# One of four graph layers: the aggregation as single 64-row graphs instead of pairs of graphs

## The chip, the cores and the metric

The kernel runs on one core of a Trainium2 chip. The metric is the device time of one execution in microseconds (us), from 2361.05 to 2364.01 in three runs, median 2362.12. A second figure, the span, runs from the first to the last instruction in one profiled execution.

The engines are named as in the profile: PE is TensorE's matmul row and PEld its weight loads, DVE is VectorE, ACT is ScalarE, POOL is GpSimd, SP is the sync engine, which issues most DMAs.

## What is computed

128 graphs of 64 nodes with 256 features go through four layers. Each adds its result to its input and normalises every row. Layer 2, to which the change belongs, is this (shapes: 128 graphs, n = 64, d = 256):

```python
A_norm = A + jnp.eye(n, dtype=A.dtype)
deg = jnp.sum(A_norm, axis=0) + jnp.sum(A_norm, axis=1) - jnp.diagonal(A_norm)
dinv = jax.lax.rsqrt(deg)
A_hat = A_norm * dinv[:, None] * dinv[None, :]
agg = jnp.einsum('nm,bmd->bnd', A_hat, features)
x = agg.reshape(-1, d)
h = jax.nn.relu(_batchnorm(x @ W1.T + b1, g1, be1))
out = h @ W2.T + b2
out = _batchnorm(out, g2, be2)
```

The change concerns the einsum alone: all 128 graphs are multiplied by one and the same 64x64 matrix `A_hat`. Layer 0 is attention over the graph, layer 1 attention over 512 listed edges, layer 3 two graph convolutions and four small LSTMs. All are in fp32.

## The kernel before

**Tiling.** The 8192 rows (128 graphs x 64 nodes) are cut into `NQ = 16` blocks. A block is a tile `[128, 4, 256]`: four groups `c` of 128 rows, and each group holds two graphs, one in partitions 0 to 63 and one in 64 to 127. A 64x64 graph matrix is therefore stored twice, on the diagonal of a 128x128 tile with zeros elsewhere: `bd` for the adjacency, and `aht` (built at line 546) for the transpose of `A_hat`.

**Stages.** Layers 0 and 1 are pipelined over the blocks, together with the end of layer 1 and the aggregation of layer 2, from the start to about 640 us. In round `q` the loop at line 560 walks through eight graphs (`l1_graph`) and puts in between: layer 0 of block `q + 2` (`l0_a` to `l0_e`), the projections of layer 1 of block `q + 1` (`l1_t`, `l1_qv`), and for block `q - 3` the three steps `v_a`, `v_b`, `v_c`. After every second block `l1_softmax` runs. The last three blocks have their `v_a`, `v_b`, `v_c` between the first batches of layer 2's first matrix product (`up_block`, line 616). Then come layer 2's products and normalisations, to about 950 us, and layer 3.

**The three steps.** `v_a` applies the attention of layer 1; its matmuls (line 351) have 64 rows and 64 columns each, and so lie in one of four quadrants of TensorE's array. `v_b` projects (line 365), adds the input and normalises by VectorE and GpSimd (line 96) into `x2`. `v_c` is the aggregation of layer 2: for each half `k` of the features and each group `c`, a 128x128 piece of `x2` is the weight operand and `aht` is streamed past it (line 377). The result is feature-major: partitions are features, columns are rows of the block. Four matmuls fill one PSUM bank, and ScalarE copies it into `A[:, q, ..]` (line 378), from which line 616 later reads.

**Banks.** PSUM banks are handed out by `bank`. The name `m`, which `v_c` uses, has three banks, taken in turn by all steps above apart from those of `l1_graph`; so the first matmul into a bank waits until the copy of its former contents has been read out. Around `v_c` these readers are ScalarE's line 264 (`spad`, from the projection), line 265 (`v`) and line 220 (`eT`). After `v_c` the banks go to lines 252 and 255 (`l1_qv`).

**Order.** The program is written as above, but a scheduler in the framework orders each engine's instructions by its own model before they are emitted, so small groups can be interleaved or moved.

Of the kernel before, what the change touches and what calls it, by code (L numbers as in the profile page):

```python
# [11 lines left out]
AF = mybir.ActivationFunctionType  # L12
# [5 lines left out]
P = 128  # L18
NB = 128
N = 64  # L20
D = 256
KD = D // P
# [5 lines left out]
PQ = 4  # L28
QT = 512
# [11 lines left out]
def kernel(ctx: ExitStack, tc: tile.TileContext, i, out):  # L41
    nc = tc.nc
# [8 lines left out]
    A = main.tile([P, NQ, 2 * QT], F32, name="A")  # L51
# [61 lines left out]
    with ExitStack() as two:  # L113
# [8 lines left out]
        def bank(shape, name="m", bufs=3):  # L122
            return (psm if name == "m" else ps).tile([P] + shape, F32, name=name, bufs=bufs)
# [22 lines left out]
        aht = wa.tile([P, P], F32, name="aht")  # L146
# [224 lines left out]

        def v_c(q):
            x2 = L1.pop(q)["x2"]
            for k in range(KD):
                p_ = bank([PQ, P])
                for c in range(PQ):
                    nc.tensor.matmul(p_[:, c, :], x2[:, c, k * P:(k + 1) * P], aht, start=True, stop=True)  # L377
                nc.scalar.activation(A[:, q, k * QT:(k + 1) * QT], p_.rearrange("p c t -> p (c t)"), AF.Copy)

        class su:  # L380

# [45 lines left out]
        for h in range(HEADS):  # L427
            r, c0 = slice((h % 2) * 64, (h % 2 + 1) * 64), P - HEADS + h
# [44 lines left out]
        for r in range(EC):  # L473
            for c in range(EC):
                nc.tensor.matmul(pcol[:, r, :], perm[:, c, r * P:(r + 1) * P], col_f[:, c, :],
                                 start=c == 0, stop=c == EC - 1)
# [83 lines left out]
        for q in range(NQ):  # L560

            between = [
                [(l0_a, q + 2), (v_a, q - LAG)],
                [(l0_b, q + 2)],
                [(v_b, q - LAG), (l0_c, q + 2)],
                [(l1_t, q + 1)],
                [(l1_qv, q + 1, 0), (l0_d, q + 2)],
                [(v_c, q - LAG)],
                [(l1_qv, q + 1, 1)],
                [(l0_e, q + 2)],  # L570
            ]
            for b in range(GQ):
                some(l1_graph, q, b)
                for step, n, *more in between[b]:
                    some(step, n, *more)
            if q % BPS == BPS - 1:
                l1_softmax(q // BPS)
# [32 lines left out]
        def pbank():  # L610
            return pools[next(banks) % len(pools)].tile([P, QT], F32, name="pz")

        def up(q, m):
            p_ = pbank()
            for k in range(KD):
                nc.tensor.matmul(p_, w1[:, k, m * P:(m + 1) * P], A[:, q, k * QT:(k + 1) * QT],  # L616
                                 start=k == 0, stop=k == KD - 1)
            nc.vector.bn_stats(st1[:, m, q, :], p_)
            return p_
# [12 lines left out]
        q = 0  # L632
        for n in range(NQ - LAG, NQ):
            for step in (v_a, v_b, v_c):
                step(n)
                up_block(q)
                q += 1
# [30 lines left out]
        for q in ends:  # L668
            p_ = up(q, 3)
# [43 lines left out]
        for q in ends:  # L713
            p_ = pbank()
# [216 lines left out]
```

## Time and profile before

| | us |
|---|---|
| median of three runs | 2362.12 |
| the profiled execution's own time | 2363.15 |
| its span | 2361.3 |
| TensorE busy in it | 2239.4 |
| VectorE busy | 1019.8 |
| ScalarE busy | 910.8 |
| GpSimd busy | 408.1 |
| mean granted TensorE clock, as a share of full speed | 0.974 |

By stretches of the span, TensorE is busy 437 of 465 us between 180 and 645 us, 111 of 115 us between 645 and 760 us, and 1376 of 1411 us from 950 us to the end. Matmuls are pipelined: a record's duration is longer than its turn on the engine, so the pace of a group is better read from the distance between starts. An fp32 matmul leaves two records[...]. In the fences below, a timeline row gives start, length, engine, line, operation, output and inputs, rows*columns of the weights, the streamed operand and the number of records; a row of a line's own view gives minimum, median and maximum duration in ns, and first and last start; a row of waits gives the total, the number and the longest.

### The profile page before, as it was taken

To read this page: it belongs to the slowest core of one execution; us is meant where nothing else is said; L and a number is where in the kernel's file an instruction comes from. 1 tells how busy PE (TensorE), PEld (TensorE's weight loads), DVE (VectorE), ACT (ScalarE), POOL (GpSimd) and SP (SyncE) were. 2 spreads that over 40 slices of the span, in tenths; PEclk is the share of its full clock that TensorE was granted. 3 is DMA by queue.
4 is the path that set the end of the run, shared out by engine and by line. 5 is a ranking of instruction groups with operands and counts; after the bars stand their busy time and mean duration, and the time that the engine had idled before them with its cause. 6 is when DMAs were issued, how large, how long until landed. Compare 5 with 4: busy or idle time off the path is not lost.

```text
span 2361.3 us, 25955 instructions
## 1 busy us (share of the span) xinstructions
PE 2239.4 (95%) x9673; PEld 1541.9 (65%) x9673; DVE 1019.8 (43%) x2320; ACT 910.8 (39%) x1885; POOL 408.1 (17%) x531
## 2 busy tenths in 40 slices
PE   5999999999899996999999999999999999999996
PEld 3767787778654444568568568568568568568475
DVE  5676766776744434322422422422422422422322
ACT  2565665566433801333333333333333333323331
POOL 1013333223320001010210210210210210210101
PEclk8899999999999997999999999999999999999998
DMA  3020222122223003000100100100100100100100
GB/s 119 10 38 29 46 57 39 38 46 39 30 47 90 0 0 116 18 18 1 54 18 1 54 18 1 54 19 1 54 18 1 54 18 1 45 10 1 36 1 27
DMA packets 126797, 74.75 MB, mean 32 GB/s; under 512 B 81872, under 2 KB 117328, under 8 KB 126416
## 3 DMA queue, kind: packets, MB, share of 16 engines
q1 hardware_dynamic: 124032, 70.22, 12.1%
q10 hardware_dynamic: 1616, 1.84, 0.2%
q8 instruction: 76, 1.25, 0.2%
q0 software_dynamic: 1024, 1.05, 0.2%
q14 instruction: 49, 0.40, 0.1%
HBM read 44.51 MB, written 28.57 MB: 31 GB/s over the span
## 4 chain that ended last, share of the span: by engine, by line
PE 87%; DVE 6%; ACT 3%; DMA 2%; POOL 2%; issue 1%; SPq 0%; POOLq 0%; ACTq 0%; DVEq 0%
PE l L818 32%; PE l L824 18%; PE g L772 5%; PE pz L680 5%; PE pz L616 5%; PE e L277 3%; PE g L780 2%; PE m L252 2%; PE m L365 2%; PE m L187 2%; PE z L286 2%; PE m L255 2%; PE m L377 1%; PE m L166 1%; DVE lo L290 1%
## 5 line engine op out<-in xcount | busy, mean ns | idle before, releaser
L818 PE MATMUL l<-H,wih 128*128 128x256 f32 (+2 forms) x2496 | 801.1, 472 | 0.3 <-DVE H L789 0.2
L818 PEld LDWEIGHTS l<-H,wih 128*128 128x128 f32 x2496 | 467.3, 191 | 246.2 <-issue 158.8
L824 PE MATMUL l<-hid,whh 128*128 128x256 f32 (+2 forms) x1536 | 435.9, 437 | 0.0
L824 PEld LDWEIGHTS l<-hid,whh 128*128 128x128 f32 x1536 | 291.8, 190 | 128.4 <-issue 61.2
L830 ACT ACTIVATE gate_i<-l,bias 128x256 f32<-128x256 f32 (+2 forms) x176 | 100.3, 570 | 646.2 <-PE l L824 514.9
L833 DVE TENSOR_TENSOR gate_i<-gate_i,gate_g 128x256 f32<-128x256 f32 (+2 forms) x96 | 47.8, 498 | 571.1 <-ACT gate_g L830 571.1
L834 POOL TENSOR_TENSOR cell<-gate_f,cell 128x256 f32<-128x256 f32 (+2 forms) x96 | 83.7, 872 | 1018.2 <-ACT gate_f L830 1018.2
L290 DVE SCALAR_TENSOR_TENSOR lo<-z,hi 128x512 fp32r<-128x512 f32 x256 | 167.4, 679 | 63.2 <-ACT hi L289 62.2
L289 ACT ACTIVATE hi<-z 128x512 fp32r<-128x512 f32 x256 | 143.7, 598 | 102.6 <-PE z L286 98.6
L82 POOL TENSOR_TENSOR ln_rs<-ln_rs,mhalf 128x2 f32<-128x2 f32 (+1 forms) x96 | 86.8, 904 | 520.3 <-DVE ln_ng L94 520.2
L830 ACT ACTIVATE gate_g<-l,bias 128x256 f32<-128x256 f32 (+2 forms) x176 | 100.2, 570 | 108.1 <-PE l L818 59.0
L830 ACT ACTIVATE gate_o<-l,bias 128x256 f32<-128x256 f32 (+2 forms) x176 | 99.5, 565 | 71.4 <-PE l L824 54.0
L277 PE MATMUL e<-lo,apad 128*128 128x512 f32 x256 | 110.7, 432 | 14.0 <-DVE lo L290 14.0
L772 PE MATMUL g<-wg,hT 128*128 128x256 f32 x512 | 122.6, 384 | 0.0
L286 PE MATMUL z<-gath_r,qs 128*128 128x512 f32 x256 | 109.9, 481 | 8.1 <-DVE lo L290 8.0
L837 DVE TENSOR_TENSOR cell<-gate_i,gate_g 128x512 f32<-128x512 f32 (+2 forms) x80 | 48.4, 604 | 154.6 <-ACT gate_g L830 154.5
L772 PEld LDWEIGHTS g<-wg,hT 128*128 128x128 f32 x512 | 98.3, 194 | 23.7 <-issue 10.5
L616 PE MATMUL pz<-A,w 128*128 128x512 f32 x256 | 112.7, 596 | 0.0
L277 PE MATMUL e<-hi,apad 128*128 128x512 f32 x256 | 108.3, 423 | 2.4 <-ACT hi L289 2.3
L838 ACT ACTIVATE gate_g<-cell 128x256 f32<-128x256 f32 (+2 forms) x176 | 89.9, 511 | 51.3 <-DVE cell L837 36.8
L843 DVE TENSOR_TENSOR H<-gate_o,gate_g 128x512 f32<-128x512 f32 (+2 forms) x80 | 47.6, 595 | 106.1 <-PE l L818 90.1
L616 PEld LDWEIGHTS pz<-A,w 128*128 128x128 f32 x256 | 48.2, 191 | 56.2 <-issue 55.0
(197 smaller groups left out, 2798.5 us busy)
## 6 DMA issues: line engine op xcount, KB each, us to landing
xin<-in_x SPq DMA_DIRECT2D x16, 512.0 KB
ld<-table SPq DMA_DIRECT2D x16, 512.0 KB
x_dram<-x SPq DMA_DIRECT2D x16, 512.0 KB
x2r<-x_dram SPq DMA_DIRECT2D x32, 256.0 KB
x_dram<-A SPq DMA_DIRECT2D x64, 128.0 KB
x3r<-x_dram SPq DMA_DIRECT2D x64, 128.0 KB
out<-st SPq DMA_DIRECT2D x64, 128.0 KB
wih<-in_WihT SPq DMA_DIRECT2D x3, 1024.0 KB
```

The costliest lines, as they stand in the source:

```text
L82: nc.gpsimd.tensor_tensor(dst, dst, mhalf[:, :n], OP.pow)
L277: nc.tensor.matmul(pes[S], apad[:, k, P - HEADS - r0:2 * P - HEADS - r0], t, start=first and n == 0, stop=False)
L286: nc.tensor.matmul(z, L1[q]["qs"][c][:, s, k * P:(k + 1) * P], gath_r, start=True, stop=True)
L289: nc.scalar.activation(hi, z, AF.Relu)
L290: nc.vector.scalar_tensor_tensor(lo, z, 0.0, hi.bitcast(F32), op0=OP.max, op1=OP.subtract)
L616: nc.tensor.matmul(p_, w1[:, k, m * P:(m + 1) * P], A[:, q, k * QT:(k + 1) * QT], start=k == 0, stop=k == KD - 1)
L680: nc.tensor.matmul(p_, w2[:, k, m * P:(m + 1) * P], hidden(q, k), start=k == 0, stop=k == M1 - 1)
L772: nc.tensor.matmul(p_[:, c, :], hT[:, k, c * P:(c + 1) * P], wg[n][:, k, :], start=k == 0, stop=k == KD - 1)
L818: nc.tensor.matmul(gates[n], wih[p][:, k, mw * P:(mw + 1) * P], Hw[:, k, :, s, :], start=k == 0, stop=not s and k == KD - 1)
L824: nc.tensor.matmul(gates[n], whh[p][:, k, m * P:(m + 1) * P], hid[:, k], start=False, stop=k == KD - 1)
L830: nc.scalar.activation(act[n], gates[n], AF.Tanh if n == "g" else AF.Sigmoid, bias=bias[:, p - 1, m:m + 1])
L838: nc.scalar.activation(act["g"], cell[:, j], AF.Tanh)
```

## The change

In `v_c` each matmul over 128 rows (two graphs) becomes two over 64 rows (one graph each, `s = 0` in partitions 0 to 63, `s = 1` in 64 to 127), with the matching 64x64 block of `aht`. Weights are then 64 rows by 128 columns, and 64 columns are streamed. The results of the two halves go to two different banks: a bank now belongs to a graph half `s` and holds both feature halves, instead of belonging to a feature half `k`. Both banks are taken at the start. ScalarE copies each bank once, into runs of 64 elements of `A`, so that `A` has the same contents as before.

```diff
         def v_c(q):
             x2 = L1.pop(q)["x2"]
+
+            p_ = [bank([KD, PQ, N]) for _ in range(2)]
             for k in range(KD):
-                p_ = bank([PQ, P])
                 for c in range(PQ):
-                    nc.tensor.matmul(p_[:, c, :], x2[:, c, k * P:(k + 1) * P], aht, start=True, stop=True)
-                nc.scalar.activation(A[:, q, k * QT:(k + 1) * QT], p_.rearrange("p c t -> p (c t)"), AF.Copy)
+                    for s in range(2):
+                        r = slice(s * N, (s + 1) * N)
+                        nc.tensor.matmul(p_[s][:, k, c, :], x2[r, c, k * P:(k + 1) * P], aht[r, r],
+                                         start=True, stop=True)
+            dst = A[:, q, :].rearrange("p (k c s t) -> p s k c t", k=KD, c=PQ, s=2)
+            for s in range(2):
+                nc.scalar.activation(dst[:, s], p_[s], AF.Copy)
```

## The prediction

> **What bounds the kernel now.** I read the page first (busy shares, then the chain), then the waits of TensorE, then the changed line, then the timeline around single blocks.
>
> ```profile
> PE 2239.4 (95%) x9673; PEld 1541.9 (65%) x9673; DVE 1019.8 (43%) x2320; ACT 910.8 (39%) x1885; POOL 408.1 (17%) x531
> PE 87%; DVE 6%; ACT 3%; DMA 2%; POOL 2%; issue 1%; SPq 0%; POOLq 0%; ACTq 0%; DVEq 0%
> ```
>
> TensorE is the path: 87% of the chain, against 6% for VectorE. The change sits in the stage from 180 to 760 us; there the waits of TensorE, asked for that stretch, are these at the top:
>
> ```profile
> PE e L277 <- DVE lo L290: 12.0, 6, 2.0
> PE z L286 <- DVE lo L290: 6.6, 8, 1.0
> PE m L377 <- POOL x L96: 2.9, 3, 1.9
> ```
>
> Some 20 us of waits for VectorE in 580 us, in a few clumps of one or two microseconds after a softmax: everywhere else TensorE has work queued. So a microsecond of TensorE more or less in the changed block is nearly a microsecond of the kernel. The changed line itself:
>
> ```profile
> L377 PEld LDWEIGHTS m<-aht,x x256: 186/192/333, 199.8 to 731.1; 128*128 128x128 f32 x128
> L377 PE MATMUL m<-aht,x x256: 270/275/580, 199.8 to 731.2; 128*128 128x128 f32 x128
> ```
>
> 16 blocks of 8 fp32 matmuls; each matmul leaves two records (two passes), so 16 a block. The durations are latencies and overlap; the pace has to be read from the timeline. Three stretches of it:
>
> ```profile
> 59.16 3.54 PEld L475 LDWEIGHTS m<-A 128*128 128x128 f32 x31 [0.24 <-issue]
> 199.81 1.86 PEld L377 LDWEIGHTS m<-aht,x 128*128 128x128 f32 x16 [0.69 <-issue]
> ...
> 700.68 1.88 PE L616 MATMUL pz<-A,w 128*128 128x512 f32 x4
> 702.40 1.95 PE L377 MATMUL m<-aht,x 128*128 128x128 f32 x16
> 704.18 1.88 PE L616 MATMUL pz<-A,w 128*128 128x512 f32 x4
> ```
>
> Line 377's loads start every (1.86 - 0.19) / 15 = 0.111 us. Line 475 loads weights of the same shape and streams only two columns past them, and its loads start every (3.54 - 0.19) / 30 = 0.112 us. So 0.11 us is what loading 128 columns of fp32 weights costs; that streaming 128 columns costs about as much is hidden under it. A block holds TensorE for 704.18 - 702.40 = 1.78 us, 28.5 us in all.
>
> [...] there is one load of 64 rows by 128 columns, at line 526, mean 310 ns, beside 200 ns for 64 by 64 at line 522, both while the granted clock was low. [...] Line 351 of this kernel already uses four 64x64 quadrants[...]:
>
> ```profile
> 659.06 1.15 PE L351 MATMUL m<-am,v 64*64 64x64 f32 x32
> 660.14 1.13 PE L616 MATMUL pz<-A,w 128*128 128x512 f32 x2
> ...
> 684.78 1.88 PE L616 MATMUL pz<-A,w 128*128 128x512 f32 x4
> 686.59 1.16 PE L351 MATMUL m<-am,v 64*64 64x64 f32 x64
> 687.68 1.98 PE L616 MATMUL pz<-A,w 128*128 128x512 f32 x4
> ```
>
> At 659 us only the upper row half works: 32 records hold TensorE for 1.08 us. At 686 us both halves alternate: 64 records in 1.09 us. The second half runs for nothing, loads included. And the switch costs: four records of line 616 last 4 x 0.43 = 1.72 us, so line 351 could have begun at 686.50 and began at 686.59 (0.09); its 16 steps at half of 0.11 us are about 0.9 of the 1.09 us (0.2 over, at the first step and at the end); the group behind it takes 1.98 instead of 1.88 us (0.10), since no weights were loaded ahead. I take 0.35 us for a switch in and out: 0.1 in (nothing where the block waits anyway), 0.05 at the first step, 0.2 out.
>
> **The change part by part.**
>
> Removed and added on TensorE: per block 8 matmuls (128 rows, 128 weight columns, 128 streamed) become 16 (64 rows, 128 weight columns, 64 streamed). Streaming halves, but the load of 128 columns stays at 0.11 us a pass, and there are twice as many. With both row halves at work, 16 / 2 matmuls x 2 passes x 0.112 = 1.79 us: the same as the 1.78 now. The arithmetic saved was never what set the pace. Added for certain is the switch, 0.35 us a block.
>
> Moved: the banks. Before, the first bank is filled (0.9 us) and then the second; now the lower half needs the second bank at once. Program order on TensorE outside the block is unchanged, but inside it the scheduler of the new program places the matmuls thus: in the five blocks n = 1, 3, .. 9 three upper ones, then three lower ones that wait for ScalarE, then alternating; in n = 2, 4, .. 10 two and two; in n = 0 four and four; in n = 11 seven and seven; in 12 to 15 alternating throughout. [...] the lower half's eight matmuls (8 x 0.224 = 1.79 us, alone enough to fill the block) start only when the second bank is free and the upper ones ahead are issued. Everything behind in TensorE's queue (lines 252 or 286) waits with them. What frees the bank stands in ScalarE's rows:
>
> ```profile
> 244.43 2.02 PE L377 MATMUL m<-aht,x 128*128 128x128 f32 x16 [0.17 <-ACT v L265]
> ...
> 275.76 1.99 PE L377 MATMUL m<-aht,x 128*128 128x128 f32 x16
> 276.38 0.17 ACT L264 ACTIVATE spad<-m 64x4 f32<-64x4 f32 x1
> ```
>
> Times from each block's present start, and the delay of what follows:
> - n = 2, 4, .. 10: the bank is freed by line 264, at 276.55 - 275.76 = 0.79 us. Lower half from about 0.88, to 2.67, switch out 2.85; now 1.75. Delay 1.1 us, five times: 5.5.
> - n = 1, 3, .. 9: the bank is freed by line 220 at 0.34 us, but the third upper matmul is issued at about 0.46. 0.46 + 1.79 + 0.2 = 2.45; now 1.86 (244.43 to 246.29). Delay 0.6, five times: 3.0.
> - n = 0: fourth upper matmul at 0.74: 2.73 against 1.78. Delay 0.95. The bank (line 264, 0.54) is no limit.
> - n = 11: line 265 frees the bank at 1.34: 1.44 + 1.79 + 0.2 = 3.43 against 2.31. Delay 1.1.
> - n = 12: it waits for GpSimd's x2 rows anyway (2.9 us above), and the last row leaves five pairs as it now leaves five matmuls. 0.3 for the switch.
> - n = 13 to 15: both banks free, 0.35 each: 1.05.
>
> Sum 5.5 + 3.0 + 0.95 + 1.1 + 0.3 + 1.05 = 11.9 us.
>
> ScalarE: two copies out as before, now into 64-element runs. Line 355 has that very pattern and takes 597 ns, line 378 599 ns: nothing. They start when the whole block is done, so the first copy comes about 0.9 us later within the block; its bank is next wanted by line 255, 0.9 us behind the block in the odd blocks and more in the even ones, and it is free about then. I book nothing, with 0.2 us a block (3 us) as the upper bound. VectorE's, GpSimd's and SP's queues keep their order. A itself holds the same values in the same places.
>
> Back the other way: VectorE, the one behind which TensorE waits after each softmax, gains room while TensorE is late. Of 20 us of such waits a tenth may vanish; but what VectorE works on there comes from TensorE after the block, so it shifts along. I take 1 us off: +11 us. The profiled execution had a span of 2361.3 and a time of 2363.15, 1.0 above the median 2362.12; the delay is added to the median: 2373.
>
> **The rivals.**
> - *Loads of the two halves don't run together with 128 columns each.* Then a block is 32 x 0.112 = 3.6 us, plus the switch: 1.8 + 0.35 = 2.15 more, some 16 x 2.15 = 34 us: 2396. For it: line 351 loads only 64 columns a quadrant. Against it: there two quadrants per row half load side by side, so both halves already load all 128 columns at once.
> - *The pace is the streaming, not the load, with 64 rows* (0.056 us a pass): the lower half takes 0.9 instead of 1.79 us. Blocks 2, 4, .. 10 are then 0.2 later, 1, 3, .. 9 and 0 about 0.3 earlier, 11 0.2 later, 13 to 15 0.5 earlier, 12 even: 1.0 - 1.8 + 0.2 - 1.5 = -2 us, 2360: no change that can be told. For it: half the rows. Against: line 475 and the 310 ns of line 526.
> - *Faster.* On that pace, and with the second bank free before the block begins (the delay of TensorE lets ScalarE get its rows 220 and 264 done first, so the waits disappear), each block saves 1.78 - 0.93 - 0.35 = 0.5 us: -8 us, 2354. It decides from a load under about 0.08 us a pass; line 475 says 0.112.
> - *Nothing changes*: the delays of the first twelve blocks vanish in the waits behind VectorE, only the switches of the last four are left, +2 us. Against: those waits sit right behind the softmax, 10 us and more after the block, on work that TensorE feeds.
>
> **How the numbers follow.** My case 0.73, 2373, with its own range 2367 to 2381: the switch 0.2 to 0.5 us a block, the copies up to 3 us, a third of the delay absorbed, and where the low-clock windows fall (from 364 to 377 us the mean granted clock is 0.87, which costs 13 x 0.13 = 1.7 us; one more or less is as much). Serial loads 0.08, 2396. Streaming pace 0.09, 2360. Faster 0.03, 2354. Absorbed 0.07, 2364. For eight in ten I reach from 2364, which takes in the absorbed case, to 2388, part of the way to the serial one; the streaming and the faster case and most of the serial one, 0.19, are left out. What can be told from no change is 0.2%, 4.7 us: slower 0.81 (my case and the serial one), same 0.16 (streaming and absorbed), faster 0.03.
>
> **What would show it.** Right: records of the new matmul line 32 a block, 64*128, starting in pairs every 0.11 us; a block of 2.2 to 2.9 us; a gap in front of the first lower matmul in n = 2, 4, .. 10; mean load still about 190 ns; line 384's copies near 599 ns. Wrong: pairs every 0.06 us or single records every 0.11 us, or TensorE's waits behind lines 290 shrinking by as much as the blocks grow.

## The result and the profile after

The changed kernel takes 2378.5 us (median of 4 runs, 2377.72 to 2379.75) against 2361.97 us before (4 runs): 16.5 us more, a ratio of 1.0069 with a 95% interval from 1.0052 to 1.0087. The forecast was 2373, the range 2364 to 2388. The profiled execution has a span of 2377.9 us, 16.6 more than before.

First the page after the change, with the busy times and the chain that ended last:

```profile
PE 2253.8 (95%) x9929; PEld 1552.5 (65%) x9929; DVE 1019.5 (43%) x2320; ACT 912.8 (38%) x1885; POOL 407.9 (17%) x531
PE 87%; DVE 6%; ACT 3%; POOL 2%; DMA 2%; issue 1%; SPq 0%; POOLq 0%; ACTq 0%; DVEq 0%
```

TensorE is busy 14.4 us longer and still carries 87% of the chain; the other engines have the same busy time within 2 us. So the loss shows on TensorE itself. Its changed line (durations in ns: minimum, median, maximum):

```profile
L380 PEld LDWEIGHTS m<-aht,x x512: 182/188/330, 199.1 to 746.7; 64*128 64x128 f32 x171
L380 PE MATMUL m<-aht,x x512: 272/272/472, 199.1 to 746.7; 64*128 64x64 f32 x171
```

Twice the records (32 a block), each as long as before: a load with half the rows takes 188 ns, where a full one took 192. A block between two rounds' work and one among line 622's matmuls (the former line 616), from the timeline of the changed kernel (start, length, and so on as explained above; other rows left out):

```profile
277.55 0.40 PE L277 MATMUL e<-lo,apad 128*128 128x512 f32 x1
...
277.88 0.52 PEld L380 LDWEIGHTS m<-aht,x 64*128 64x128 f32 x4 [0.36 <-issue]
277.88 2.72 PE L380 MATMUL m<-aht,x 64*128 64x64 f32 x32
...
278.39 0.17 ACT L264 ACTIVATE spad<-m 64x4 f32<-64x4 f32 x1
...
278.61 1.86 PEld L380 LDWEIGHTS m<-aht,x 64*128 64x128 f32 x28 [0.21 <-ACT spad L264]
...
280.53 0.50 PE L286 MATMUL z<-gath_r,qs 128*128 128x512 f32 x1
...
690.06 1.86 PEld L380 LDWEIGHTS m<-aht,x 64*128 64x128 f32 x32 [0.76 <-POOL x L96]
690.06 2.00 PE L380 MATMUL m<-aht,x 64*128 64x64 f32 x32
...
691.99 0.30 PEld L622 LDWEIGHTS pz<-A,w 128*128 128x128 f32 x2
```

In the one at 690 us both halves run side by side: 32 loads in the same 1.86 us in which line 377 did 16, a load every (1.86 - 0.19) / 31 = 0.054 us, so one every 0.108 us in each half. In the one at 277 us, two upper matmuls (4 records) are issued, then TensorE stands until ScalarE's line 264 has emptied the second bank at 278.56. The six upper matmuls still to come, whose bank is free, don't pass the waiting one: no load of the block starts between the fourth record and 278.61. The lower half starts at 278.61 with all its 16 passes still to do, and sets the end.

The waits of TensorE in the stretch from 180 to 775 us (total, number, longest):

```profile
PE e L277 <- DVE lo L290: 12.0, 6, 2.0
PE z L286 <- DVE lo L290: 7.7, 8, 1.3
PE m L380 <- POOL x L96: 2.9, 3, 2.0
```

The second was 6.6 us before, in a stretch of nearly the same length: it grew by 1.1, where I had taken 1 off. Last, the granted clock right behind softmaxes, by windows of 8 us (columns: window, length, busy time and records of PE, PEld, DVE, ACT and POOL, then PEclk, DMA share, GB/s). Three of the kernel before, then the corresponding three of the changed one:

```profile
292.00:300.00 8.00, 7.00 (x21) 5.18 (x22) 7.82 (x12) 3.04 (x6) 3.22 (x5) 0.57 0.22 66
370.00:378.00 8.00, 7.76 (x35) 5.56 (x35) 7.91 (x11) 4.49 (x8) 1.80 (x3) 0.79 0.20 68
...
520.00:528.00 8.00, 6.56 (x18) 4.85 (x19) 7.82 (x11) 2.80 (x5) 3.65 (x5) 0.57 0.22 66
```

```profile
294.00:302.00 8.00, 6.00 (x19) 4.19 (x18) 7.82 (x11) 2.96 (x6) 4.49 (x5) 0.57 0.23 64
372.00:380.00 8.00, 6.00 (x18) 4.12 (x16) 7.82 (x11) 2.96 (x6) 4.54 (x5) 0.57 0.24 65
...
529.00:537.00 8.00, 6.22 (x17) 4.54 (x18) 7.82 (x12) 2.80 (x5) 3.99 (x5) 0.57 0.27 66
```

The clock's records in these two traces hold only the shares 1 and 0.5, so a PEclk of 0.79 is a half-speed stretch of 3.4 us in the window ((1 - 0.79) x 2 x 8), and 0.57 one of 6.9 us. Behind the six softmaxes between 200 and 640 us the kernel before has two long ones and four short ones, the changed kernel five long ones and one short one.

### The profile page after: what moved, and what is told of

The parts are those of the page before. It is cut to its first block, busy times and chain, and to the rows that moved or that the text cites. A ratio compares the mean times of both kernels' runs of the same rounds, so it can differ in the third digit from the quotient of the medians.

```text
span 2377.9 us, 26465 instructions
## 1 busy us (share of the span) xinstructions
PE 2253.8 (95%) x9929; PEld 1552.5 (65%) x9929; DVE 1019.5 (43%) x2320; ACT 912.8 (38%) x1885; POOL 407.9 (17%) x531
## 4 chain that ended last, share of the span: by engine, by line
PE 87%; DVE 6%; ACT 3%; POOL 2%; DMA 2%; issue 1%; SPq 0%; POOLq 0%; ACTq 0%; DVEq 0%
PE l L824 32%; PE l L830 18%; PE pz L622 5%; PE g L778 5%; PE pz L686 5%; PE e L277 4%; PE g L786 2%; PE m L252 2%; PE m L365 2%; PE m L187 2%; PE z L286 2%; PE m L255 2%; PE m L380 2%; PE m L228 1%; PE m L166 1%
```

## The experiments

The theory: the load of 128 weight columns sets the pace, so halving rows and streamed columns saves nothing; the loss is the switch of tiling (0.35 us a block) plus the delay of the lower half by the order and by the second bank's wait. The rivals: streaming sets the pace; the halves don't overlap; the loss is the clock's.

**1. What TensorE time in the block is worth (`dose3`).** The kernel before, with the block's first matmul issued three more times.

```diff
-                    nc.tensor.matmul(p_[:, c, :], x2[:, c, k * P:(k + 1) * P], aht, start=True, stop=True)
+                    for _ in range(4) if c == 0 and k == 0 else range(1):
+                        nc.tensor.matmul(p_[:, c, :], x2[:, c, k * P:(k + 1) * P], aht, start=True, stop=True)
```

> The kernel before, with three full-size matmuls of the aggregation repeated in each of the 16 blocks (same bank, same result; no row tiling, same bank order). TensorE gets 16 x 3 x 0.224 = 10.7 us of work, about what the change added to its blocks (10 us). Theory A, that a lengthened round also lengthens the windows of low granted clock behind the softmax: more than the dose, 2374 to 2381 us, and the low-clock time between 140 and 760 us rises from 34 us towards the 51 us of the changed kernel. Theory B, that the excess belongs to the row tiling itself: the dose alone, 2372 to 2373 us, low-clock time about 34 us.

Measured: 2372.12 us against 2362.73, ratio 1.0039 [1.0024, 1.0053]. 3 matmuls x 2 passes x 0.111 x 16 blocks are 10.7 us; 9.4 arrived. So a microsecond in the block is nearly one of the kernel, and this longer round brought no further loss: between 140 and 770 us the clock was low for 31 us (34 in the kernel before, 51 in the changed one).

**2. The switch alone (`switch1`).** The kernel before with one extra matmul of 64 rows ahead of each block, whose result is overwritten.

```diff
+                if k == 0:
+                    nc.tensor.matmul(p_[:, 0, :N], x2[:N, 0, :P], aht[:N, :N], start=True, stop=True)
```

> The kernel before, with one extra 64-row matmul (64 rows, 128 weight columns, 64 streamed) ahead of each block's first matmul, whose result the block then overwrites. If a switch of the tiling mode in and out costs about 0.35 us: 16 x (0.22 + 0.35) = 9 us more, about 2371 us or somewhat above. If the switch costs nothing and the matmul its two passes alone: 16 x 0.22 = 3.6 us more, about 2365.5 us.

Measured: 2370.5 us, 7.8 more than before (1.0032 [1.002, 1.0045]). Its timeline around one block:

```profile
276.70 0.40 PE L277 MATMUL e<-lo,apad 128*128 128x512 f32 x1
277.02 0.43 PE L377 MATMUL m<-aht,x 64*128 64x64 f32 x2
277.39 2.05 PE L379 MATMUL m<-aht,x 128*128 128x128 f32 x16
```

The block begins 0.32 us after the last matmul ahead of it (0.23 to 0.24 where no switch lies between, as in experiment 5), and the full-row matmuls start 0.37 later: 0.22 for the extra matmul's two passes and 0.15 for the way in and out. The whole 7.8 us are 0.49 a block: 0.22 for the two passes and 0.27 for the switch. The switch is real; its size here is a little below the 0.35.

**3. Quadrants (`quad`).** The changed kernel with each matmul cut again, into two of 64 weight columns, in the same banks and the same place.

```diff
-                    for s in range(2):
-                        r = slice(s * N, (s + 1) * N)
-                        nc.tensor.matmul(p_[s][:, k, c, :], x2[r, c, k * P:(k + 1) * P], aht[r, r],
-                                         start=True, stop=True)
+                    for j in range(2):
+                        for s in range(2):
+                            r = slice(s * N, (s + 1) * N)
+                            f0 = k * P + j * N
+                            nc.tensor.matmul(p_[s][j * N:(j + 1) * N, k, c, :], x2[r, c, f0:f0 + N], aht[r, r],
+                                             start=True, stop=True)
```

> The changed kernel with each 64-row matmul cut once more, into two of 64 weight columns, in the four quadrants of the array; banks and waits as in the changed kernel. If the load of 128 columns sets the changed kernel's pace, a pass now takes 0.056 us in each quadrant: the last three blocks fall from 2.1 to about 1.3 us, the blocks that wait for their second bank by 0.9 us, in all 16 x 0.85 = 13 us less than the changed kernel or a little more with the clock windows, 2360 to 2365 us. If a matmul has a fixed cost of about 0.11 us a pass whatever its columns, no gain: 2378 us.

Measured: 2365.42 us, ratio to before 1.0013 [1.0004, 1.0022]; 13 us less than the changed kernel. The same arithmetic, the same streams of 64 columns, twice the instructions; only each load is of 64 columns instead of 128 (median 135 ns, 188 in the changed kernel). Its timeline shows the same wait for line 264, and the rest in 1.15 us instead of 1.9:

```profile
276.06 0.44 PE L382 MATMUL m<-aht,x 64*64 64x64 f32 x6
276.79 1.15 PE L382 MATMUL m<-aht,x 64*64 64x64 f32 x58 [0.29 <-ACT spad L264]
277.87 0.73 PE L286 MATMUL z<-gath_r,qs 128*128 128x512 f32 x2
```

The pace was the load of 128 columns. "Streaming sets the pace" falls.

**4. One half after the other (`apart`).** The changed kernel with all eight upper matmuls ahead of the eight lower ones (the loop over `s` outermost).

> The changed kernel with the order turned: all eight matmuls of the upper half, then all eight of the lower half, so that the halves never work side by side. If the halves overlap in the changed kernel and the load sets the pace: a block takes 16 x 0.224 + 0.35 = 3.9 us, 34 us above the kernel before, 2396 us, or up to 2402 with longer low-clock windows. If they hardly overlap in the changed kernel: about the changed kernel's 2378 us.

Measured: 2402.61 us (2398.38 to 2414.27), 1.0184 [1.0158, 1.0209]. Serial halves cost 24 us more than alternating ones (2378.5), so in the changed kernel they do overlap. (The clock is low for 58 us here against 51 there, which at half speed explains 3.4 of the 24 us at most.) Not foreseen was where the clock gave way: see experiment 7.

**5. Another place (`late_before`, `late_after`, `late_quad`).** In each round `v_c` is called two slots later, where its banks have long been free; the same edit to the kernel before, to the changed one, and to the one with quadrants.

```diff
-                [(v_c, q - LAG)],
+                [],
                 [(l1_qv, q + 1, 1)],
-                [(l0_e, q + 2)],
+                [(v_c, q - LAG), (l0_e, q + 2)],
```

> The kernel before, with its step v_c called two slots later in each round (directly ahead of l0_e instead of after the second graph batch): same matmuls, other place. It is the yardstick for the next two. If the place costs nothing by itself, 2362 (2359 to 2365). If the rows that v_c follows there keep TensorE waiting, or if what came after v_c lacks its cover, up to 2370.

> The changed kernel with v_c at that later place, where both banks are free long before the block. Theory 'the second bank's wait makes two thirds of the loss, the tiling switch one third': the upper half no longer runs alone, each block costs only a switch more, 16 x 0.35 = 5.6 us above late_before, that is about 2368 and 8 to 11 us below the changed kernel. Rival 'the loss is the halves themselves (loads of 128 columns by one half don't keep the pace of 0.111 us, or the clock gives way after blocks of half rows)': the place doesn't matter, 14 to 17 us above late_before, about 2378.

> As late_after, but each matmul cut again into two of 64 weight columns, so that four quadrants of TensorE work. Load time a block 32 x 2 passes / 4 quadrants x 0.056 = 0.9 us instead of 1.79 plus the switch of 0.35: 0.5 us less a block than late_before, 8 us in sum: 2354 if late_before is at 2362, faster than both kernels. Rival 'the quadrants' gain is taken back at the next wait for VectorE': 2360 to 2362.

Measured against 2361.55 before: `late_before` 2356.82 (0.998 [0.9971, 0.9988]), `late_after` 2363.88 (1.001 [1.0002, 1.0018]), `late_quad` 2355.99 (0.9975 [0.9965, 0.9985]).

The place alone gains 4.7 us, which I had not expected of the control. The waits of `late_before` in the same stretch say where from:

```profile
PE e L277 <- DVE lo L290: 12.0, 6, 2.0
PE z L286 <- DVE lo L290: 3.6, 9, 0.5
PE m L377 <- POOL x L96: 2.9, 3, 1.9
```

Line 286's wait for VectorE falls from 6.6 to 3.6 us, and line 377's wait for ScalarE's `v` (1.5 us before) is gone: 4.5 us in sum. The tally isn't exact: line 187 now waits 1.2 us for VectorE, line 351's waits fall by 0.8, and the clock is low for 3.4 us less.

At this place the change costs 7.1 us (5.6 were expected) instead of 16.5, 0.44 a block. The timelines of `late_before` and of `late_after` around the same block:

```profile
322.50 0.39 PE L277 MATMUL e<-lo,apad 128*128 128x512 f32 x1
322.73 1.95 PE L377 MATMUL m<-aht,x 128*128 128x128 f32 x16
324.51 0.81 PE L228 MATMUL m<-wh,eT 128*128 128x256 f32 x3
```

```profile
323.57 0.40 PE L277 MATMUL e<-lo,apad 128*128 128x512 f32 x1
323.90 2.00 PE L380 MATMUL m<-aht,x 64*128 64x64 f32 x32
325.83 1.99 PE L228 MATMUL m<-wh,eT 128*128 128x256 f32 x8
```

From the last matmul ahead to the first behind it is 2.01 us and 2.26 us: 0.25 more, and the switch is all of it. No matmul waits for a bank. So 9.4 of the 16.5 us belong to the old place: to the order inside the block, the second bank's wait, and what hangs on them. About 6 of them are in the blocks themselves (without block 12, the change adds 9.8 us to them at the old place and 3.7 here); most of the rest is the clock's, as experiment 7 shows. No run tells the order and the wait apart. "The place doesn't matter" (2378) falls.

With quadrants the same stretch takes 1.62 us:

```profile
323.41 0.40 PE L277 MATMUL e<-lo,apad 128*128 128x512 f32 x1
323.73 1.16 PE L382 MATMUL m<-aht,x 64*64 64x64 f32 x64
325.03 1.99 PE L228 MATMUL m<-wh,eT 128*128 128x256 f32 x8
```

That is 0.39 less than `late_before`, 6.2 us over 16 blocks, and yet the two kernels can't be told apart: this expectation missed. In the two profiles, line 286's waits for VectorE are 1.0 us longer (4.6), line 351's for GpSimd 1.0 longer (2.1), and 1.8 us are lost before the first block begins, where the kernels do the same work (the first 140 us have a clock of 0.88 in one and 0.90 in the other). Where the rest of the medians' difference went is not settled. Both versions beat the kernel before by 0.2 to 0.25%.

**6. Load and stream apart (`halves`, `late_cols`).** `halves` is the kernel before with each matmul cut in its streamed columns, so that the same 128x128 weights are loaded twice. `late_cols` is `late_before` with each cut in its weight columns, so that half as much is loaded, twice, and 128 columns are streamed past it each time.

```diff
-                    nc.tensor.matmul(p_[:, c, :], x2[:, c, k * P:(k + 1) * P], aht, start=True, stop=True)
+                    for s in range(2):
+                        r = slice(s * N, (s + 1) * N)
+                        nc.tensor.matmul(p_[:, c, r], x2[:, c, k * P:(k + 1) * P], aht[:, r], start=True, stop=True)
```

```diff
-                for c in range(PQ):
-                    nc.tensor.matmul(p_[:, c, :], x2[:, c, k * P:(k + 1) * P], aht, start=True, stop=True)
+                for j in range(2):
+                    for c in range(PQ):
+                        f0 = k * P + j * N
+                        nc.tensor.matmul(p_[j * N:(j + 1) * N, c, :], x2[:, c, f0:f0 + N], aht, start=True, stop=True)
```

> The kernel before with each matmul of v_c cut in its streamed columns: the same 128x128 weights loaded twice, 64 columns streamed each time; full rows, so no switch of tiling and no second bank. Theory 'the load of 128 columns sets the pace, 0.111 us a pass': 32 x 0.111 = 3.57 us a block instead of 1.78, 16 x 1.79 = 28.6 us more: 2391 (2387 to 2393). Rival 'streaming sets the pace': 32 x 0.056 = 1.79 us, 2362. If low-clock windows come from half the rows standing idle and not from long loads, no new window is seen right behind these blocks.

> late_before with each matmul cut in its weight columns: 128 rows, 64 weight columns, 128 streamed, first all left halves and then all right ones of a bank. If streaming 128 columns takes a pass about 0.107 us by itself, 32 x 0.107 = 3.4 us a block instead of 1.8, and 16 x 1.65 = 26 us more than late_before: 2383, plus the switch (0.35 a block, 5.6): 2389. If streaming is quicker (0.056): 2362. If the clock gives way where half of the array's cells stand idle, be it rows or columns, low-clock stretches behind the blocks; if only rows count, none.

`halves`: 2388.75 us, 1.0111 [1.0096, 1.0126], 27.2 more than before where the load's theory said 28.6. Its block, from its timeline, is (3.68 - 0.28) / 31 = 0.110 us a pass with 64 columns streamed:

```profile
278.55 3.68 PE L379 MATMUL m<-aht,x 128*128 128x64 f32 x32
```

`late_cols`: 2370.3 us, 1.0039 [1.0025, 1.0054], 13.5 more than `late_before`; between my two values, so this expectation missed. Two stretches of one block explain it, each from a narrow view of its timeline:

```profile
283.54 0.82 PE L379 MATMUL m<-aht,x 128*64 128x128 f32 x6
...
284.03 1.15 PE L379 MATMUL m<-aht,x 128*64 128x128 f32 x16
```

At the start one column half works alone, a pass every (0.82 - 0.27) / 5 = 0.11 us: that is the stream of 128 columns, with only 64 loaded. Later it is (1.15 - 0.27) / 15 = 0.059, since the neighbouring groups of the two column halves run at the same time. So in these runs loading 128 columns (`halves`, 0.110) and streaming 128 columns (0.11) each took a pass of 0.11 us by themselves, and the matmul of the kernel before is balanced: the pace fell only where both were halved, in the quadrants of `late_quad`, to 4 x (1.16 - 0.22) / 63 = 0.060 us a pass in each of the four. The column halves' overlap across groups is what I had left out.

**7. The clock (`after_again`, `late_apart`).** `after_again` is the changed kernel once more; `late_apart` is `late_after` with the upper eight matmuls ahead of the lower eight.

> The changed kernel once more, for a second look at its low-clock stretches. Theory 'the longer low-clock stretches after its softmaxes (5 of 6 lasted 6.8 us, against 2 of 6 in the kernel before) belong to the change': again 5 or 6 of 6, and mean clock 0.95 between 200 and 640 us. Rival 'phase of the clock's own window': another number, near 2 or 3, with 0.97. The time in both cases 2377 to 2380.

> late_after with the eight upper matmuls ahead of the eight lower ones, so that for 3.3 us a block only half of TensorE's rows work at a time. Block 3.65 us against 2.26: 16 x 1.4 = 22 us more than late_after, 2386. Theory 'a stretch in which only half the rows work counts as idle for the clock': several new low-clock stretches of 3.4 us right behind blocks, each 1.5 us more, up to 2402. Rival 'the clock doesn't look at the rows; the stretches seen behind such blocks come from their stalls': none behind blocks, 2384 to 2388.

`after_again`: 2377.89 us, 1.0066 [1.0049, 1.0083]. All six of its stretches behind softmaxes are long (0.57 in each window of 8 us); two of the six windows, the rest alike:

```profile
373.00:381.00 8.00, 6.75 (x19) 4.99 (x20) 7.82 (x12) 2.80 (x5) 3.45 (x5) 0.57 0.23 66
452.00:460.00 8.00, 7.28 (x23) 5.43 (x24) 7.82 (x12) 3.17 (x6) 3.02 (x4) 0.57 0.24 66
```

So 11 of 12 are long in two profiles, and not in these alone: the eight timed executions of the changed kernel have a mean clock of 0.972 or 0.973, and none of 52 of the kernel before is below 0.974. In `late_after`, with the same matmuls, all six are short (0.79). The longer ones therefore don't come from half rows as such, but go with the old place.

The clock's records in the traces show what the length goes with. In the profiles of before and after, all low-clock stretches but the last, which ends with the record, last whole steps of 3.41 us (one step to five, 3.41 to 17.07 us) and start a whole number of such steps apart: those behind the last five softmaxes of the changed kernel at 294.38, 372.88, 451.39, 529.90 and 608.40 us, 23 steps each time, and each lasts two steps, 6.83 us. What differs is how far into its step the softmax falls, taken here by the start of its first scan, line 307 (one starts at 293.31 us, 2.34 us behind the step at 290.97). In the eight profiles with the aggregation at the old place, each with these six softmaxes, it starts 1.04 to 2.36 us into the step at all 24 long stretches, and at all 24 short ones before 1.00 or after 2.41.

Two rounds of the kernel before take 76.0 to 77.1 us, 22 to 23 steps, and so the scan moves from softmax to softmax: 0.43, 1.46, 2.85, 0.29, 1.20, 3.22 us into the step. Two rounds of the changed kernel take 77.7 to 78.7 us, close to 23 steps (78.5), and the scan moves little and settles: 3.14, 2.34, 1.88, 1.54, 1.33, 1.33, and in `after_again` 1.1 to 1.4 throughout. So I read these stretches as no property of its matmuls: the change makes two rounds about 1.6 us longer in their blocks, a long stretch adds some 0.7, and that length holds the softmaxes where the stretch becomes long. At the later place only 3 of 30 are long, at 1.3 to 1.7 us. A run with the changed kernel's block and another length of round was not made.

`late_apart`: 2394.78 us (1.0144 [1.0127, 1.0161]), 30.9 more than `late_after`, of which some 16 x 1.39 = 22 are the longer blocks (3.65 instead of 2.26). The clock is low for 51 us between 140 and 770 us instead of 31, which at half speed is up to 10 us more. Here it does give way behind blocks. A block and the time behind it, first in `late_apart`, then in `halves`, whose full-row block is as long:

```profile
408.00:412.00 4.00, 4.00 (x36) 3.58 (x35) 1.35 (x3) 2.32 (x8) 3.53 (x2) 1.00 0.16 61
412.00:416.00 4.00, 4.00 (x12) 3.17 (x12) 1.85 (x5) 0.92 (x2) 0.33 (x1) 0.57 0.00 0
```

```profile
404.00:408.50 4.50, 4.33 (x37) 3.92 (x36) 1.97 (x4) 3.77 (x8) 0.00 (x0) 1.00 1.66 136
408.50:412.00 3.50, 3.50 (x19) 3.12 (x19) 1.27 (x3) 1.75 (x6) 2.04 (x2) 1.00 0.43 140
```

In `late_apart` TensorE is busy for the whole 4 us and the clock still drops to half right after; in `halves` it stays at 1.00. The drop follows 12 of the 30 blocks of `apart` and `late_apart` (block 12 left out, which waits for GpSimd within itself in all kernels). The steps tell which: at each of these 12, at least 2.7 us of the block lie within one step; at the other 18 it is 2.5 us at most, apart from one with 2.74. In `halves`, full-row blocks fill up to 3.4 us of a step, and none is followed by a drop. Nor are the shorter blocks of `late_cols` (2.3 us) and of `late_after` (1.7 us, both halves at work). In the changed kernel a drop is seen behind the first block, whose halves run alone for much of 2.3 us; in `after_again` that block has none.

```profile
199.00:202.00 3.00, 2.87 (x34) 2.79 (x35) 1.89 (x3) 2.67 (x6) 0.00 (x0) 1.00 0.00 0
202.00:205.60 3.60, 3.60 (x10) 2.79 (x9) 0.79 (x2) 1.27 (x4) 0.00 (x0) 0.53 0.01 2
```

## Why the prediction was right, and what it missed

The delays by blocks, measured from the start of the last matmul ahead of a block to the start of the first behind it, in the profiles of before and after:

| blocks | forecast delay, us | before | after | delay |
|---|---|---|---|---|
| 0 | 0.95 | 2.66 | 3.40 | 0.74 |
| 1, 3, .. 9 | 0.6 | 2.43 | 2.89 | 0.46 |
| 2, 4, .. 10 | 1.1 | 1.98 | 2.98 | 1.0 |
| 11 | 1.1 | 2.72 | 3.74 | 1.02 |
| 12 | 0.3 | 7.32 | 7.35 | 0.03 |
| 13 to 15 | 0.35 | 2.21 | 2.45 | 0.24 |

With their numbers of blocks these make 9.8 us. The forecast counted a tenth of a microsecond more in the group behind each block, 1.6 us in all: its first load starts together with its matmul (both at 691.99 us behind the block at 690 us; in the kernel before the load starts at 704.08 us, the matmul at 704.18). In `late_after` eight matmuls of line 228 take 1.99 us; the like eight in the kernel before took 1.89. The eight stretches between blocks without a softmax are indeed 0.08 to 0.14 us longer each, 0.8 together; behind the even blocks the group of line 286 takes only 0.02 more. That is 10.7 against a sum of 11.9.

- *The pace is the load, nothing is saved by half the rows*: right, by `quad` and `halves`. In `late_apart` the upper half alone, with 64 rows, loads every (1.08 - 0.19) / 8 = 0.11 us, as full rows do (0.111).
- *Streaming 128 columns costs about as much*: right, by `late_cols`.
- *Both halves overlap*: right, by the timeline at 690 us and by `apart`.
- *The switch, 0.35 us a block*: about right. 0.25 in the block plus 0.1 behind it in `late_after`, 0.27 in `switch1`.
- *The second bank's wait and the order delay the lower half*: right in its place and size, by the timeline at 277 us (lower half from 0.73 after the block's start; 0.88 was forecast) and by `late_after`, which is without them.
- *ScalarE's copies cost nothing*: nothing speaks against it; line 384 has a median of 595 ns, line 378 had 599.
- *A microsecond comes back from the waits behind VectorE*: it did not. Line 286's waits even grew by 1.1 us. But the two stretches between blocks that hold a softmax and the same length of low clock in both kernels (behind blocks 2 and 8) are 0.02 and 0.18 us shorter than before, so these waits cost next to nothing as well.
- *The low-clock stretches move, one more or less is 1.7 us*: wrong in that it was put down to chance and kept out of the sum. Between 140 and 770 us the clock is low for 34.1 us before and for 51.2 us in both profiles of the changed kernel: five steps more, three or four of them behind softmaxes, one behind block 12, and in the first profile one behind block 0. In that profile they lie in the stretches behind blocks 0, 4, 6, 10 and 12, and just these five are longer by 1.46, 0.67, 0.72, 1.57 and 1.45 us: 5.9 in all (5.5 in `after_again`).

Blocks and the groups behind them 10.7, these five stretches 5.9, the two with an unchanged clock -0.2, and 0.2 ahead of the first block and behind the last one: that is the 16.6 us by which the span grew. So about two thirds of the loss have the forecast cause in the forecast size. The term that was mis-sized is the clock's, nothing instead of 5.9 us, and the microsecond taken off made it 1 worse. That 2378.5 still lies in the range is owed in part to its width, in which I had counted one such step and not five. That the clock took the 5.9 us is read from two pairs of profiles; no run changed the clock alone.

What makes the clock fall was not shown. A single long wait can't be the whole of it: behind the softmaxes none was longer than 2.0 us, and in `late_apart` the clock fell behind 4 us in which TensorE was never without a matmul.

## What to carry to other kernels

Cutting a matmul into halves of rows saved no time here, since what set its pace was not cut: the load of 128 columns and the stream of 128 columns both took 0.11 us, and only quadrants halved both (0.060 in each). A block in another tiling was paid for on the way in and out (0.27 us in `switch1`, 0.35 in `late_after`), so it should be long, or, which wasn't tried, lie beside other work of the same tiling.

When outputs are redistributed over banks so that the second bank is needed at once, look at who empties it and what is queued behind the waiting matmul: in the block at 277 us TensorE issued nothing past the waiting matmul until 0.73 us after the block's start, and the order and the wait together cost more than the switch (about 6 us of the blocks' 9.8). Moving the same block by two slots took away 9.4 of the 16.5 us, and by itself made the kernel before 4.7 us faster.

Where the clock falls behind a stall that returns in every second round, look at the length of the round too: here two rounds of 77.7 to 78.7 us, close to 23 of the clock's steps (78.5), went with stalls that settled at one place in the step and with two steps at half speed, and two rounds of 76.0 to 77.1 us with stalls that moved and, in four of six, one step. That the length is the cause is my reading, as said above.

## What the runs showed of the hardware that was not expected

- In the profiles of before and after the clock changed only on steps of 3.41 us. The same stall went with one step at half speed or two by where it lay: in the eight profiles with the aggregation at the old place, two at all 24 softmaxes whose scan starts 1.04 to 2.36 us into a step, and one at the other 24, within 200 to 640 us.
- A stretch in which only half of TensorE's rows work at a time was followed by half the clock, in `late_apart` at 412 us after 4 us in which TensorE was busy for 4.00: in `apart` and `late_apart` behind 12 of 30 blocks, all with at least 2.7 us in one step, while full-row blocks of 3.6 us in `halves` were followed by none. Whether half the columns would do the same isn't known: in `late_cols` one column half works alone for about half a microsecond only, at each end of a block.
- Matmuls in the two column halves with full rows also ran at the same time: in `late_cols` a pass every 0.059 us, where one column half alone takes 0.11.
